# The front of a routed layer, rewritten as a loop in a held order, with rows gathered six tiles ahead and one-hots in 16 bits

## The chip, the core and the metric

The kernel runs on one core of a Trainium2 chip. The metric is device time in microseconds (us), the median of several executions. Engines are named as in the profile: PE is the matrix engine, PEld its weight loads, DVE the vector engine, ACT the scalar engine, POOL the one that issues the gathers here, and SP the one that issues most other DMAs. PEclk is the clock granted to PE as a share of full speed.

## What is computed

`x` has 32 items of 64 rows and 512 columns in fp32, that is 2048 rows, kept as NT = 16 tiles of 128 rows. Four layers follow each other, each of them `x = x + ffn(cond(x))`. What the change touches is the seam between layers 0 and 1:

```python
# layer 0, the end: a mixture of 7 experts, top 2, and a shared expert
shared = (silu(x @ sh_gate) * (x @ sh_up) / 8) @ sh_down
y0 = shared + sum(w[e] * expert_ffn(x, r_gate[e], r_up[e], r_down[e]) for e in range(7))
# layer 1, the start: a 64x64 mix per item, chosen by subject, then a router
c = einsum("bct,bcd->bdt", x, weights[subjects])
logits = c @ gate_w.T + gate_b          # 32 experts
topk_logits, topk_idx = top_k(logits, 4)
...
```

After this the rows of `c` are sorted by expert, each of the 32 experts works on its rows, and the results go back to their rows with softmax weights. Layer 2 (an adapter and a soft mixture) and layer 3 (paged attention and a quantised linear) come later and are not touched.

## The kernel before

`layer0` ends with its routed experts, which leave their rows in DRAM (`ys`). Behind a branch that treats rows beyond an expert's capacity, `layer1` (L1409) runs its front, a loop over the 16 tiles. For tile `i` it does this:

- `combined` (L1190) gathers two rows per row of the tile from `ys` (`gather`, L336, an indirect DMA that POOL issues) into `yk`, of which there are six buffers, and adds each to `x` with its gate (L1198, DVE). SP stores `x` to DRAM for later (L1430).
- One matmul with a block-diagonal weight mixes the items (L1432, into PSUM tile `mm`, 128x512). ACT copies it to `c` (L1436), and SP stores `c` to `rows` (L1437), from where the experts will gather.
- Four transposes of `c` go to `tp` (L1440), ACT copies them to `cT` (L1442), and four matmuls with `cT` as the stationary side and 32 moving columns make the router's logits `rp` (L1447). Four tiles share one PSUM bank for `rp`. DVE adds the bias (`lg`, L1449), and `choose` takes the largest eight values and their indices (L901, L902).
- The shared expert of layer 0 is still missing in six late tiles (8 to 13, the list `todo`). Its first part `up` (L481: 16 matmuls in fp32, which the hardware runs as 32) is in the even steps and `down` in the odd ones (L487: an identity matmul that brings `x` into PSUM at L492, two matmuls at L495, and a copy by ACT back over `x` at L496).
- `put` (L904) works on groups of tiles, given by `groups`: one step after the last tile of a group, it makes the place of every row among the rows of its expert. DVE makes a one-hot of the choice (`hot`), sums it (`sel`, L916) and accumulates it (`pre`, L918). Two matmuls give the rows ahead of each one (`at`, L921), and `placed` (L1238) turns a place into a tile number `tl` and a row `row`. From these, DVE makes two one-hot matrices `a` and `b` (L1254). ACT scales `a` by the row's number (L893, in `total`), four matmuls per tile sum a table of row numbers in PSUM (L895), and DVE adds the table to `tokens` (L896). The table, `at` and `fixed` are three stretches of one PSUM bank, `tok`.

When all 16 tiles are through, `end` (L1260) selects from `tokens` the row numbers of the two experts that have a fixed place (`fixed`). `m.ready` then starts to gather their rows (`xr<-rows,fixed`, L336), and `m.run` runs the experts. The weights of the first two experts are asked for just ahead of `end`, and `rest` (L1373) loads the tiles 8 to 15 of `x` in one go, at the start of the front.

The order of instructions on an engine is chosen by a scheduler from the dependences in the program. Only instructions that are pinned one by one hold the order in which the program issues them; in the front before, these are loads and a few others. The heart of the loop is:

```python
groups = {3: 4, 7: 4, 11: 4, 13: 2, 14: 1, 15: 1}
for i in range(NT):
    x = combined(sb, i, 3, bridge.x[i])
    nc.sync.dma_start(out=xs[i * P : (i + 1) * P, :], in_=x)
    o = ps.tile([P, D], F32, name="mm", tag="mm")
    nc.tensor.matmul(o, bridge.weights[i], x, start=True, stop=True)
    if i % 2 == 0 and i // 2 < len(todo):
        shared.up(sb, ps, todo[i // 2])
```

Of the kernel before, what the change touches and what calls it, by code (L numbers as in the profile page):

```python
# [2 lines left out]

# [38 lines left out]
LATER = range(6, NT - 2)  # L42
GAP = 2
# [35 lines left out]
def _consts():  # L79
# [14 lines left out]

    b["iota"] = np.tile(np.arange(P, dtype=f), (P, 1))
# [21 lines left out]
    d["same32"] = (p[:, None] % 32 == e).astype(f)  # L117
# [109 lines left out]

class Prog:


    def __init__(self, tc, a, ctx):
# [3 lines left out]
        self.named = {}  # L235
        self.constants(self.const, "cst")
# [222 lines left out]
class Shared:  # L459
# [12 lines left out]
    def up(self, sb, ps, i, tag="sh"):  # L472
# [13 lines left out]
        l0_expert(g, sb, self.acts[i], gu[:, 0:2, :], gu[:, 2:4, :], None)  # L486

# [290 lines left out]
class Moe:  # L778
# [297 lines left out]
    def run(self, xs, per_tile):  # L1076
# [138 lines left out]
        combined.fetch = fetch  # L1215
# [3 lines left out]
class Ranked(Moe):  # L1219
# [3 lines left out]
    def begin(self, sb, bank, at):  # L1223
        nc, g = self.g.nc, self.g
        self.bank, self.at = bank, at
        nc.vector.memset(self.pre[:, 0], 0.0)  # L1226
        self.tok = self.keep.tile([TC1, P], F32, name="tokens1")
        nc.vector.memset(self.tok, 0.0)
        self.room = self.keep.tile([P, 2, E1], F32, name="room1")
        self.widx = self.keep.tile([P, E1], I32, name="widx1")  # L1230
        self.each = self.keep.tile([P, E1], I32, name="each1")
        self.fixed = self.keep.tile([P, FIXED1 * 320 // P], I32, name="fixed1")
# [5 lines left out]
    def placed(self, sb, hot, i, n):  # L1238

        nc, iota, K = self.g.nc, self.g.c("iota"), self.K  # L1240
        fi, place = self.chosen[:, i : i + n, :], self.place[:, i : i + n, :]
        nc.vector.tensor_reduce(place, hot, AX.X, ALU.add)
        ai = sb.tile([P, n, K], I32, name=f"ai{n}")
        nc.vector.tensor_copy(ai, place)
        nc.vector.tensor_single_scalar(ai, ai, 7, ALU.arith_shift_right)
        tl = sb.tile([P, n, K], F32, name=f"tl{n}")
        nc.vector.tensor_copy(tl, ai)
        row = sb.tile([P, n, K], F32, name=f"row{n}")
        nc.vector.scalar_tensor_tensor(row, tl, -float(P), place, ALU.mult, ALU.add)
        nc.vector.scalar_tensor_tensor(tl, tl, 32.0, fi, ALU.mult, ALU.add)  # L1250
        a_ = sb.tile([P, n * K, TC1], F16, name=f"a_{n}", bufs=1)
        b_ = sb.tile([P, n * K, P], F16, name=f"b_{n}", bufs=1)
        for o, w, v in ((a_, TC1, tl), (b_, P, row)):
            nc.vector.tensor_tensor(  # L1254
                o, iota[:, 0:w].unsqueeze(1).to_broadcast([P, n * K, w]),
                v.rearrange("p n k -> p (n k)").unsqueeze(2).to_broadcast([P, n * K, w]), ALU.is_equal,
            )
        self.total(self.bank[0:TC1, 0:P], self.tok, a_, b_, a_, i, n)

    def end(self, sb):  # L1260

        g, nc, E, tok, ident = self.g, self.g.nc, self.E, self.tok, self.g.ident
        fixed = self.bank[:, 128:133]
# [97 lines left out]
class Bridge:  # L1361
# [11 lines left out]
    def rest(self, pool):  # L1373
        for i in range(NT):
            if i not in self.x:
                self.x[i] = self.g.load_x(pool, self.xs, i, NT - len(EARLY), True)
# [31 lines left out]

def layer1(g, bridge, combined, beside, w2):  # L1409
    tc, nc, a = g.tc, g.nc, g.a  # L1410
    with ExitStack() as ctx:
# [4 lines left out]
        with ExitStack() as c1:  # L1416
# [5 lines left out]
            bank, rps = (ps.tile([P, 512], F32, name=k, tag=k, bufs=1) for k in ("tok", "rp"))  # L1422
            m.begin(sb, bank, bank[:, 256:384])
            shared, todo = bridge.shared, list(LATER[GAP:])
            bridge.rest(wp)

            groups = {3: 4, 7: 4, 11: 4, 13: 2, 14: 1, 15: 1}
            for i in range(NT):
                x = combined(sb, i, 3, bridge.x[i])
                nc.sync.dma_start(out=xs[i * P : (i + 1) * P, :], in_=x)  # L1430
# [1105 lines left out]
```

## Time and profile before

| what | us |
|---|---|
| median of 3 runs | 2584.26 (2582.10 to 2585.11) |
| the profiled execution | 2621.27, of it 2619.4 in the span |
| layer 0 with its experts, to the branch | 0 to 599.9 |
| layer 1's front, which the change rewrites | 599.9 to 729.5 |
| layer 1's experts and what leads to layer 2 | 729.5 to 1230 |
| layers 2 and 3 | 1230 to 2619 |

PE is busy for 97.1 of the 129.6 us of the front, DVE for 73.5, ACT for 34.8 and POOL for 33.8, at a mean PEclk of 0.81. In all the other stages of the table PE is busy between 91 and 97 per cent of the time. The times of a stage come from the trace, whose span starts at 0; a row of the trace that reads `607.44 0.59 ACT L1436` starts at 607.44 us and lasts 0.59 us, and what stands in brackets at its end is the time for which the engine was idle just before, and what ended it.

### The profile page before, as it was taken

The page shows a single profiled execution, that of the slowest core. Times are in us where ns is not written, and L with a number is a line of the kernel's source. Part 1 is how long each engine was busy: PE and PEld are TensorE (multiplying, and loading weights), DVE is VectorE, ACT ScalarE, POOL GpSimd, SP SyncE. Part 2 cuts the span into 40 slices and gives each one's busy share as a digit, 9 for nine tenths or more (in the row PEclk, how much of TensorE's full clock was granted, in tenths as well). Part 3 has the DMA queues.
Part 4 walks back from the last instruction along what each step waited for, and adds up shares of the span by engine and source line. Part 5 has one row for each costly group of instructions (what it writes and reads, how often), then busy time and mean ns, then how long its engine had stood idle before and what let it go on. Part 6 is the DMA issues. An engine that isn't in the chain of part 4 may idle for free.

```text
span 2619.4 us, 42294 instructions
## 1 busy us (share of the span) xinstructions
PE 2460.3 (94%) x16512; PEld 1622.1 (62%) x16527; DVE 1413.2 (54%) x3457; ACT 723.7 (28%) x1513; POOL 901.5 (34%) x955
## 2 busy tenths in 40 slices
PE   6999989998789999978999999999999999979998
PEld 4777766666556666746666666666666665435554
DVE  4666646824645554436544444444444432658786
ACT  2445421112211111102222222222222221246664
POOL 2223226604044443523333333333333312564440
PEclk9999979998789999989999999999999999989999
DMA  2335235535356976844222222222222313524441
GB/s 101 114 119 181 87 107 181 185 130 189 136 165 224 361 272 242 292 130 147 68 74 71 71 71 71 72 74 75 71 73 72 95 54 133 166 64 125 129 145 44
DMA packets 132566, 339.34 MB, mean 130 GB/s; under 512 B 23993, under 2 KB 25049, under 8 KB 125056
## 3 DMA queue, kind: packets, MB, share of 16 engines
q1 hardware_dynamic: 90720, 188.83, 21.1%
q0 software_dynamic: 41056, 141.89, 17.3%
q10 hardware_dynamic: 576, 5.77, 0.5%
q8 instruction: 134, 2.20, 0.3%
q14 instruction: 80, 0.66, 0.1%
HBM read 245.21 MB, written 107.22 MB: 135 GB/s over the span
## 4 chain that ended last, share of the span: by engine, by line
PE 42%; DVE 9%; issue 1%; POOL 1%; DMA 1%; ACT 0%; ACTq 0%; POOLq 0%; SPq 0%; DVEq 0%
PE out L1909 9%; PE lp L1766 7%; PE gp L1898 3%; PE pp L2223 3%; PE zp L1843 3%; PE yp L1711 2%; PE hp L1875 2%; PE y L2471 2%; PE op L2449 2%; PE pT L2424 2%; PE sp L2402 1%; DVE xt L1213 1%; PE ep L1852 1%; DVE inv L1802 1%; PE kp L2375 1%
## 5 line engine op out<-in xcount | busy, mean ns | idle before, releaser
L1124 PE MATMUL gu<-xT,wt 128*128 128x320 f32 (+3 forms) x1472 | 396.8, 417 | 0.8 <-issue 0.8
L1124 PEld LDWEIGHTS gu<-xT,wt 128*128 128x128 f32 x1472 | 276.6, 192 | 120.5 <-issue 52.9
L1909 PE MATMUL out<-sb_w,gT 128*128 128x512 f32 x512 | 234.1, 600 | 10.3 <-DVE nn L1746 6.6
L1766 PEld LDWEIGHTS lp<-xnT,sb_mu 128*128 128x128 f32 x2048 | 234.8, 193 | 9.2 <-issue 6.7
L1766 PE MATMUL lp<-xnT,sb_mu 128*128 128x128 f32 x2048 | 237.8, 276 | 2.1 <-DVE xnT L308 1.4
L1843 PE MATMUL zp<-sb_w,xnT 128*128 128x512 f32 x512 | 228.4, 595 | 4.3 <-DVE z L1845 4.3
L1136 PE MATMUL y<-wt,hT 128*128 128x512 f32 (+2 forms) x544 | 201.2, 598 | 2.8 <-DVE yo L1144 2.2
L336 POOL DMA_INDIRECT kvst<-kv,gidx x96 | 96.6, 1006 | 279.0 <-DMA oldkv<-kvst 196.6
L1902 DVE COPY gT<-gp 128x512 f32<-128x512 f32 x64 | 44.3, 692 | 250.1 <-PE gp L1898 249.7
L1909 PEld LDWEIGHTS out<-sb_w,gT 128*128 128x128 f32 x512 | 93.6, 191 | 115.7 <-issue 95.5
L1843 PEld LDWEIGHTS zp<-sb_w,xnT 128*128 128x128 f32 x512 | 93.7, 190 | 112.2 <-issue 100.8
L336 POOL DMA_INDIRECT yk<-ys,slot x96 | 97.8, 1019 | 145.2 <-DVE pre L1226 74.2
L336 POOL DMA_INDIRECT kvt<-newkv,oidx x96 | 100.8, 1050 | 132.2 <-DMA kvt<-oldkv 73.0
L1880 ACT ACTIVATE h<-hp 128x512 f32<-128x512 f32 x128 | 69.5, 594 | 218.8 <-PE hp L1875 218.6
L1136 PEld LDWEIGHTS y<-wt,hT 128*128 128x128 f32 (+2 forms) x544 | 73.0, 167 | 65.5 <-issue 52.9
L336 POOL DMA_INDIRECT xr<-rows,stok x101 | 98.2, 973 | 44.2 <-issue 18.2
L774 POOL TENSOR_TENSOR ga<-ga,sg 128x288 f32<-128x288 f32 (+3 forms) x64 | 50.7, 793 | 169.3 <-ACT sg L770 168.2
L1920 POOL TENSOR_TENSOR xt<-xt,bc_bias 128x512 f32<-128x512 f32 x16 | 20.3, 1266 | 222.8 <-DMA x<-xt 208.9
L1771 DVE TENSOR_TENSOR lT<-lp,cmu 128x512 f32<-128x512 f32 x64 | 43.6, 680 | 93.7 <-PE lp L1766 93.7
L1804 POOL TENSOR_TENSOR eT<-eT,inv 128x512 f32<-128x512 f32 x64 | 71.8, 1124 | 55.1 <-DVE inv L1803 32.0
L1898 PEld LDWEIGHTS gp<-lT,h 128*64 128x64 f32 x2048 | 65.8, 139 | 38.7 <-issue 26.5
L1795 ACT ACTIVATE eT<-eT 128x512 f32<-128x512 f32 x64 | 40.4, 631 | 174.0 <-DVE eT L1792 151.8
(430 smaller groups left out, 4673.4 us busy)
## 6 DMA issues: line engine op xcount, KB each, us to landing
ys<-yo SPq DMA_DIRECT2D x106, 256.0 KB
oldkv<-kvst SPq DMA_DIRECT2D x96, 224.0 KB
kvt<-oldkv SPq DMA_DIRECT2D x96, 224.0 KB
ys<-zero SPq DMA_DIRECT2D x10, 2048.0 KB
xt<-x SPq DMA_DIRECT2D x62, 256.0 KB
x<-xt SPq DMA_DIRECT2D x48, 256.0 KB
wt<-w_e SPq DMA_DIRECT2D x7, 1536.0 KB
sb_w<-w SPq DMA_DIRECT2D x5, 1024.0 KB
```

The lines of the kernel that those rows point to most:

```text
L336: ins = self.nc.gpsimd.indirect_dma_start(out=out, out_offset=None, in_=src, in_offset=bass.IndirectOffsetOnAxis(ap=idx, axis=0), **kw)
L1124: follow(nc.tensor.matmul(o, wj[:, c, ic * P : (ic + 1) * P], xTs[u][:, c, 0:n], start=c == 0, stop=c == 3))
L1136: follow(nc.tensor.matmul(y[row : row + n, :], hTs[e][:, ic, col : col + n], wd[:, ic, :], start=ic == 0, stop=ic == 1,))
L1711: g.first(c, nc.tensor.matmul(yp, self.xT[:, c, :], w["w_2"][:, c, :], start=c == 0, stop=False))
L1766: g.first(e + c, nc.tensor.matmul(lp[:, e, :], w["mu"][:, c, (4 * q + e) * P : (4 * q + e + 1) * P], self.xnT[:, c, :], start=c == 0, stop ...
L1804: g.pin(nc.gpsimd.tensor_tensor(e3, e3, inv.unsqueeze(2).to_broadcast([P, 8, T]), ALU.mult))
L1843: g.first(c, nc.tensor.matmul(zp, self.xnT[:, c, :], w["w1"][:, c, cols], start=c == 0, stop=c == 3))
L1875: g.first(e + b, nc.tensor.matmul(hp[:, b, e, :], self.ews[q][r, e, :], self.z[q][r, e * P : (e + 1) * P], start=True, stop=True))
L1880: g.pin(nc.scalar.activation(self.hs[q][b], hp[:, b], AF.Gelu))
L1898: g.first(e + b + k, nc.tensor.matmul(gp[r, e, cols], self.hs[q][b][:, e, r], self.lT[q][:, e, cols], start=True, stop=True))
L1909: g.first(e, nc.tensor.matmul(self.out, self.gTs[q][:, e, :], w["w2"][:, 4 * q + e, :], start=q + e == 0, stop=q + e == 6 and q == 3))
L2223: nc.tensor.matmul(pp, xT[i][:, c, :], (w["w_kv3"] if z else wq)[:, c, :], start=c == 0, stop=c == 3)
```

## The change

The loop becomes a class, `Mixed`, whose `run` issues one step per tile and one more. What it issues goes through `g.held`, a wrapper which pins every instruction, so that each engine keeps the order of the program.

- **Gathers.** `fetch` asks for the two `yk` of a tile six tiles ahead (`LEAD`); there are 14 buffers. The adds of tile `s+1` and its store stand behind the mix of tile `s`.
- **Shared expert.** `pieces` cuts it into six pieces for each tile: four quarters of `up` and two halves of `down`. Three pieces go into each step until none is left. The identity matmul goes; ACT copies the result to `sht`, and POOL adds that to `x`.
- **Router.** For the tiles 0 to 10 (`SPLIT`), the weights are the stationary side, and the four partial products go side by side to the four column tiles of PE (`parts`, 32 rows each). ACT copies them, and one matmul with a constant (`same32`, which moves to another group of constants) sums them to `rp`. The other tiles use the form before.
- **Groups.** `put` is a generator that halts where its next part belongs to another engine; the loop takes it up again at given points. The last groups are {13: 2, 15: 2}. The one-hots are made from 16-bit operands in a layout with the choice `k` innermost, DVE scales `a` in place of ACT, and the tile number comes from adding and subtracting a large constant instead of integer steps. The sum over `k` becomes two adds.
- **Banks.** The table accumulates over all 16 tiles in a PSUM bank of its own. `at` (with `fixed`), `rp`, `parts`, `mm` and `tp` have one bank each, and the shared expert has two.
- **Loads.** `rest` loads one tile of `x` per step, two before the loop. The weights of the first two experts are asked for in the steps 10 and 12.

```diff
+LEAD = 6
+GROUPS = {3: 4, 7: 4, 11: 4, 13: 2, 15: 2}
+SPLIT = range(11)
...
+class Ordered:
+    def __getattr__(self, name):
+        issue = getattr(self.engine, name)
+
+        def ordered(*args, **kw):
+            ins = issue(*args, **kw)
+            self.g.pin(ins)
+            return ins
+
+        return ordered
...
+    def pieces(self, sb, ps, todo, x):
+        nc, w = self.g.held, self.w
+        gus, sgs, ys, acts = {}, {}, {}, {}
+        def up(i, q):
+            j, ic = q // 2, q % 2
+            if q == 0:
+                gus[i] = ps.tile([P, 4, P], F32, name="gu", tag="sh")
+            for c in range(4):
+                nc.tensor.matmul(
+                    gus[i][:, q, :], w["w_sh"][:, c, j * 256 + ic * P : j * 256 + ic * P + P], self.hT[i][:, c, :],
+                    start=c == 0, stop=c == 3,
+                )
+            if q == 3:
+                sgs[i] = sb.tile([P, 2, P], F32, name="sg")
+                nc.scalar.activation(sgs[i], gus[i][:, 0:2, :], AF.Sigmoid)
+        def act(i):
+            gu, sg = gus.pop(i), sgs.pop(i)
+            nc.vector.scalar_tensor_tensor(sg, gu[:, 0:2, :], 0.125, sg, ALU.mult, ALU.mult)
+            acts[i] = sb.tile([P, 2, P], F32, name="hT")
+            nc.vector.tensor_tensor(acts[i], gu[:, 2:4, :], sg, ALU.mult)
+        def down(i, ic):
+            if ic == 0:
+                ys[i] = ps.tile([P, D], F32, name="y", tag="sh")
+            nc.tensor.matmul(ys[i], acts[i][:, ic, :], w["w_shd"][:, ic, :], start=ic == 0, stop=ic == 1)
+            if ic:
+                t = sb.tile([P, D], F32, name="sht", bufs=2)
+                nc.scalar.copy(t, ys[i])
+                nc.gpsimd.tensor_tensor(x[i], x[i], t, ALU.add)
+        on_pe = []
+        for k, i in enumerate(todo):
+            for q in range(4):
+                if q == 2 and k:
+                    on_pe += [(partial(down, todo[k - 1], ic), None) for ic in range(2)]
+                on_pe.append((partial(up, i, q), partial(act, i) if q == 3 else None))
+        on_pe += [(partial(down, todo[-1], ic), None) for ic in range(2)]
+        return on_pe
...
-    def begin(self, sb, bank, at):
+    def begin(self, sb, ps):
         nc, g = self.g.nc, self.g
-        self.bank, self.at = bank, at
         nc.vector.memset(self.pre[:, 0], 0.0)
+        self.iota = sb.tile([P, P, K1], F16, name="iota16", bufs=1)
+        nc.vector.tensor_copy(self.iota, g.c("iota").unsqueeze(2).to_broadcast([P, P, K1]))
+        self.table = ps.tile([TC1, P], F32, name="table", bufs=1)
...
+    def put(self, sb, ps, i, n):
+        g, nc, K, E = self.g, self.g.held, self.K, self.E
         fi, place = self.chosen[:, i : i + n, :], self.place[:, i : i + n, :]
+        nc.vector.tensor_copy(fi, self.idx[:, i : i + n, 0:K])
+        shape = [P, n, K, E]
+        hot = sb.tile(shape, F32, name=f"hot{n}", bufs=2)
+        nc.vector.tensor_tensor(
+            hot, g.c("iota")[:, 0:E].unsqueeze(1).unsqueeze(1).to_broadcast(shape),
+            fi.unsqueeze(3).to_broadcast(shape), ALU.is_equal,
+        )
+        half = sb.tile([P, n, 2, E], F32, name=f"half{n}", bufs=1)
+        nc.vector.tensor_tensor(half, hot[:, :, 0:2], hot[:, :, 2:4], ALU.add)
+        sel = sb.tile([P, n, E], F32, name=f"sel{n}", bufs=2)
+        nc.vector.tensor_tensor(sel, half[:, :, 0], half[:, :, 1], ALU.add)
+        for j in range(n):
+            nc.vector.tensor_tensor(self.pre[:, i + j + 1], self.pre[:, i + j], sel[:, j], ALU.add)
+        at = ps.tile([P, 4, E], F32, name="at", bufs=1)[:, 0:n]
+        yield "tensor"
+        nc.tensor.matmul(at, g.ones, self.pre[:, i : i + n], start=True, stop=False)
+        nc.tensor.matmul(at, g.c("upper"), sel, start=False, stop=True)
+        yield "vector"
+        nc.vector.tensor_tensor(hot, hot, at.unsqueeze(2).to_broadcast(shape), ALU.mult)
         nc.vector.tensor_reduce(place, hot, AX.X, ALU.add)
+        tile_ = sb.tile([P, n, K], F32, name=f"tile{n}", bufs=2)
+        nc.vector.tensor_scalar(tile_, place, 1.0 / P, 0.5 / P - 0.5, ALU.mult, ALU.add)
+        nc.vector.tensor_scalar(tile_, tile_, MAGIC, MAGIC, ALU.add, ALU.subtract)
+        row = sb.tile([P, n, K], F16, name=f"row{n}", bufs=2)
+        nc.vector.scalar_tensor_tensor(row, tile_, -float(P), place, ALU.mult, ALU.add)
+        tl = sb.tile([P, n, K], F16, name=f"tl{n}", bufs=2)
+        nc.vector.scalar_tensor_tensor(tl, tile_, 32.0, fi, ALU.mult, ALU.add)
+        yield "vector"
+        a_ = sb.tile([P, n, TC1, K], F16, name=f"a_{n}", bufs=2)
+        b_ = sb.tile([P, n, P, K], F16, name=f"b_{n}", bufs=2)
+        for o, w, v in ((b_, P, row), (a_, TC1, tl)):
+            to = [P, n, w, K]
             nc.vector.tensor_tensor(
+                o, self.iota[:, 0:w].unsqueeze(1).to_broadcast(to), v.unsqueeze(2).to_broadcast(to), ALU.is_equal
             )
+        for j in range(n):
+            nc.vector.tensor_scalar(a_[:, j], a_[:, j], g.c("tok")[:, i + j : i + j + 1], None, ALU.mult)
+        yield "tensor"
+        for j in range(n):
+            for k in range(K):
+                nc.tensor.matmul(
+                    self.table, a_[:, j, :, k], b_[:, j, :, k], start=i + j + k == 0,
+                    stop=i + j == NT - 1 and k == K - 1,
+                )
...
+    def end(self, ps):
+        g, nc, tok, ident = self.g, self.g.held, self.tok, self.g.ident
+        nc.vector.tensor_copy(tok, self.table)
+        fixed = ps.tile([P, FIXED1 * 320 // P], F32, name="fixedp", tag="at", bufs=1)
...
-    def rest(self, pool):
-        for i in range(NT):
-            if i not in self.x:
-                self.x[i] = self.g.load_x(pool, self.xs, i, NT - len(EARLY), True)
+    def rest(self, pool, i):
+        if i < NT and i not in self.x:
+            self.x[i] = self.g.load_x(pool, self.xs, i, NT - len(EARLY), True)
...
+class Mixed:
...
+    def fetch(self, i):
+        if i >= NT:
+            return
+        g, m = self.g, self.before
+        self.yk[i] = [self.sb.tile([P, D], F32, name="yk", bufs=K0 * (LEAD + 1)) for _ in range(K0)]
+        for k, yk in enumerate(self.yk[i]):
+            g.gather(yk, m.ys, m.slot[:, i, k : k + 1], later=True)
+    def adds(self, i):
+        if i >= NT:
+            return
+        g, x = self.g, self.bridge.x[i]
+        for k, yk in enumerate(self.yk.pop(i)):
+            g.held.vector.scalar_tensor_tensor(x, yk, self.before.gates[:, i, k : k + 1], x, ALU.mult, ALU.add)
+        g.held.sync.dma_start(out=self.xs[i * P : (i + 1) * P, :], in_=x)
+    def mix(self, i):
+        nc = self.g.held
+        o = self.ps.tile([P, D], F32, name="mm", bufs=1)
+        nc.tensor.matmul(o, self.bridge.weights[i], self.bridge.x[i], start=True, stop=True)
+        self.c[i] = self.sb.tile([P, D], F32, name="c")
+        nc.scalar.copy(self.c[i], o)
+        nc.sync.dma_start(out=self.m.rows[i * P : (i + 1) * P, :], in_=self.c[i])
+    def turn(self, i):
+        nc, c = self.g.held, self.c.pop(i)
+        tp = self.ps.tile([P, 4, P], F32, name="tp", bufs=1)
+        for cc in range(4):
+            nc.tensor.transpose(tp[:, cc, :], c[:, cc * P : (cc + 1) * P], self.g.ident)
+        self.cT[i] = self.sb.tile([P, 4, P], F32, name="cT", bufs=2)
+        nc.scalar.copy(self.cT[i], tp)
+    def route(self, i):
+        nc, cT = self.g.held, self.cT.pop(i)
+        if i not in SPLIT:
+            self.rp[i] = self.ps.tile([P, E1], F32, name="rp", bufs=1)
+            for cc in range(4):
+                nc.tensor.matmul(self.rp[i], cT[:, cc, :], self.wr[:, cc, :], start=cc == 0, stop=cc == 3)
+            return
+        parts = self.ps.tile([P, P], F32, name="parts", bufs=1)
+        for cc in range(4):
+            nc.tensor.matmul(parts[32 * cc : 32 * cc + 32], self.wr[:, cc, :], cT[:, cc, :], start=True, stop=True)
+        self.parts[i] = self.sb.tile([P, P], F32, name="partss", bufs=2)
+        nc.scalar.copy(self.parts[i], parts)
+    def logits(self, i):
+        if i in SPLIT:
+            self.rp[i] = self.ps.tile([P, E1], F32, name="rp", bufs=1)
+            self.g.held.tensor.matmul(self.rp[i], self.parts.pop(i), self.g.c("same32"), start=True, stop=True)
+    def choose(self, i):
+        lg = self.sb.tile([P, E1], F32, name="lg")
+        self.g.held.vector.tensor_tensor(lg, self.rp.pop(i), self.br, ALU.add)
+        self.m.choose(i, lg)
+    def run(self):
+        g, m, bridge, puts = self.g, self.m, self.bridge, []
+        todo = list(LATER[GAP:])
+        for i in todo[:2]:
+            bridge.rest(self.wp, i)
+        pieces = bridge.shared.pieces(self.sb, self.ps, todo, bridge.x)
+        def acts():
+            while self.late:
+                self.late.pop(0)()
+        def fill(n=1):
+            for piece, late in pieces[:n]:
+                if len(pieces) <= 2:
+                    acts()
+                piece()
+                if late:
+                    self.late.append(late)
+            del pieces[:n]
+        def go(engine):
+            for put in list(puts):
+                if put[1] == engine:
+                    put[1] = next(put[0], None)
+                    if put[1] is None:
+                        puts.remove(put)
+        for i in range(LEAD):
+            self.fetch(i)
+        fill(4)
+        self.adds(0)
+        for s in range(NT + 1):
+            self.fetch(s + LEAD)
+            bridge.rest(self.wp, todo[0] + 2 + s)
+            if s < NT:
+                self.mix(s)
+            self.adds(s + 1)
+            fill()
+            if s:
+                self.logits(s - 1)
+            if s < NT:
+                self.turn(s)
+            acts()
+            if s:
+                self.choose(s - 1)
+            fill()
+            go("tensor")
+            go("vector")
+            if s == NT - 1:
+                go("vector")
+            if s < NT:
+                self.route(s)
+            fill()
+            if s - 1 in GROUPS:
+                puts.append([m.put(self.sb, self.ps, s - GROUPS[s - 1], GROUPS[s - 1]), "vector"])
+                go("vector")
+            if s in (10, 12):
+                m.weights((s - 10) // 2)
+        while puts:
+            go("tensor")
+            go("vector")
+        assert not pieces
+        m.end(self.ps)
...
+            m.begin(sb, ps)
+            Mixed(g, sb, ps, wp, m, combined.moe, bridge, wr, br, xs).run()
```

## The prediction

> **What bounds the stage.** I read first the page's engine row (PE 94% busy over the span), then a table by stage, which says where PE is not busy. The changed code runs from 599.9 us (first instruction behind the branch that closes layer 0) to 729.5 us (first row gather of layer 1's experts). All times of the trace are us from the span's start.
>
> ```profile
> span 2619.4 us, 42294 instructions
> ...
> PE 2460.3 (94%) x16512; PEld 1622.1 (62%) x16527; DVE 1413.2 (54%) x3457; ACT 723.7 (28%) x1513; POOL 901.5 (34%) x955
> ```
>
> ```profile
> core 0: us, PE busy (x) PEld busy (x) DVE busy (x) ACT busy (x) POOL busy (x), PEclk, DMA share, GB/s
> 599.90:624.50 24.60, 15.36 (x66) 10.18 (x66) 9.28 (x19) 4.11 (x8) 16.16 (x16) 0.80 0.75 231
> 624.50:676.50 52.00, 50.69 (x324) 39.95 (x323) 32.49 (x89) 15.29 (x28) 17.62 (x16) 0.96 0.53 177
> 676.50:708.70 32.20, 24.24 (x124) 17.76 (x124) 20.92 (x65) 12.75 (x22) 0.00 (x0) 0.76 0.39 150
> 708.70:729.50 20.80, 6.85 (x37) 5.58 (x36) 10.80 (x41) 2.61 (x5) 0.00 (x1) 0.50 0.22 74
> ```
>
> Four parts, four limits: a start with a hole in it; a middle where PE is full; a late part with holes and a PE clock of 0.76; and 20.8 us after the last expert choice in which PE is busy 6.85 us at half clock. In the last part one short chain runs, three times over: one-hots on DVE, their scaling on ACT, the table's matmuls, the add into `tokens`, and only then the next group's prefix sums, because all of them share one PSUM bank. Two turns of it in the timeline:
>
> ```profile
> 719.45 0.68 DVE L1254 TENSOR_TENSOR b<-sb_cst,row 128x512 f16<-128x512 f32 x1
> 720.05 0.55 DVE L1254 TENSOR_TENSOR a<-sb_cst,tl 128x384 f16<-128x384 f32 x1
> 720.64 0.61 ACT L893 ACTIVATE a<-a,sb_cst 128x384 f16<-128x384 f16 x1 [5.20 <-DVE a L1254]
> 721.30 0.45 PEld L895 LDWEIGHTS <-a 128*96 128x96 f16 x4 [3.85 <-ACT a L893]
> ...
> 722.00 0.28 DVE L896 TENSOR_TENSOR tokens<-tokens,tok 96x128 f32<-96x128 f32 x1 [1.40 <-PE tok L895]
> 722.34 0.50 PEld L921 LDWEIGHTS tok<-pre,sb_cst 128*128 128x128 f32 x2 [0.59 <-DVE tokens L896]
> ...
> 729.50 0.95 POOL L336 DMA_INDIRECT xr<-rows,fixed  x1 [57.66 <-DVE yo L1293]
> ```
>
> The hole of the start is one wait, on ACT, and PE stands behind it:
>
> ```profile
> 607.44 0.59 ACT L1436 COPY c<-mm 128x512 f32<-128x512 f32 x1 [2.42 <-issue]
> 616.72 0.59 ACT L1442 COPY cT<-tp 128x512 f32<-128x512 f32 x1 [8.70 <-DMA yk<-ys,slot]
> 617.36 1.78 PEld L1447 LDWEIGHTS rp<-sb_w_r,cT 128*128 128x128 f32 x8 [8.05 <-issue]
> ```
>
> The copy's source (tp) was done by 609.3, so the releaser named is not its producer. The DMA view has no packet of an instruction queue between 602 and 616, and one at 616 to 617, with the DMA engines at a share near 0.95 (gathers): I read the wait as an instruction fetch of ACT that came late. PE's clock is then 0.50 from 616.7 to 628.0 (windows).
>
> [...] 2048 elements took 2288 ns, 1536 took 1752. For 16 bits no row exists[...] The trace has such matmuls in layer 2: 32 of `csum` (128\*32) in 1.08 us against 8 of `rp` in 0.97 us. [...] Here PE stood from 676.5 to 680.5 and the clock was 0.50 for 680 to 688. [...]
>
> **PE prices** (full clock, from start to start in the timeline of 630 to 641): mm 0.86 us for 512 columns; four transposes tp 0.45; rp 0.89; an up quarter 32/4 = 8 instructions of 0.113 = 0.90; one half of down 0.86. Before, two tiles took 630.24 to 640.91 = 10.67, that is 5.33 a tile, with nothing idle.
>
> **Part by part.**
>
> *Shared expert.* Three pieces a step, as before (six per two tiles), so 3 x 0.89 = 2.67. The identity matmul (L492, 0.9 us per tile of six) goes: -5.4 us of PE. In its place ACT copies to `sht` (0.59, as for L496) and POOL adds it to x (1.27, as L1920 has it). POOL then has 2 gathers x 1.25 + 0.7 = 3.2 us a step, hidden.
>
> *Router as column tiles, 11 steps.* rp 0.89 becomes parts, 8 of 0.03 = 0.25, and logits, 2 of 0.11 = 0.22; with two drains of 0.2 about 0.15 saved. ACT gets one copy of 128x128 (0.25, as L2452).
>
> *A step.* 0.86 + 2.67 + 0.45 + 0.47 + 0.2 = 4.65 us; the puts' share is (0.45 + 16 x 0.09)/4 = 0.47 a tile. Sum 5.1, I take 5.05. ACT's waits fit: turn needs mix + 0.2 + 0.59, and PE has 1.1 us of fill and logits there; route needs 1.33 from the turn's start, and has 0.45 + 0.90.
>
> *DVE.* Two adds 2 x 0.75 and gaps = 1.57; choose (0.19 + 0.19 + 0.09 + 0.19 and gaps) 0.75; the activation 0.88 every other step. A put of four: cast, hot, half, sel, four pre = 0.18 + 0.69 + 0.42 + 0.29 + 0.88 = 2.6 with gaps (the reduce of 1.05 goes); hot x at, place, four small = 2.3; one-hots 1.22 + 0.96 and four scalings of about 0.2 = 3.0. Sum 7.9, before 9.3 and 2.13 on ACT. Per tile 1.57 + 0.75 + 0.44 + 2.0 = 4.8: just below PE. If 16 bits bring nothing: 2.29 + 1.75 + 4 x 0.46 = 5.9, per tile 5.5, so DVE would set the pace. Below nothing it can't go: the elements stay. I take the fast value. A mix needs its adds, which stand first in the step before: from logits (1.8 us into a step) through choose, the longest piece and the next adds is 1.8 + 0.75 + 3.0 + 1.57 = 7.1 of the 10 us that two steps give.
>
> *Table in a bank of its own.* The `tokens` add (0.28) and the wait between groups go. The table's operands are read with a stride of 8 bytes, of which the trace shows nothing[...]. I take 0.09.
>
> *Gathers six tiles ahead.* 12 gathers go out back to back, 600.3 to 615.3. Tile 1 was in by 608.0 before; the loop needs it by 611. Later tiles have slack, so DVE's waits for yk (13.7 us in sum) go. In the first 30 us the queues carry 24 gathers, 12 stores and six of the x loads (SP had all eight x loads out by 566; now six stand in the loop): 42 x 0.26 MB = 11 MB, 365 GB/s, more than the 320 to 340 seen. Stores and loads slip, which costs nothing with this lead; an instruction fetch may slip too.
>
> **The sum.** First mix at 606.3 as before (it hangs on the first two gathers, landed at 604.1 and 605.4). Eleven steps of 5.05, less one piece: 661.0. Steps 11 to 14 have no pieces and run the chain mix 0.86 + 0.2, copy 0.59, tp 0.7, copy 0.59, rp 0.94 = 3.9, say 4.0: step 15 starts at 677. DVE is behind there (step 14 has adds 1.57, choose 0.75, 3.0 and the next group's 1.75): choose(15) ends 8.0 us into step 15. Then for the last two tiles 1.75, prefix sums 1.4 at half clock, 1.6, 1.65, table 1.5, copy, four selecting matmuls and fixed 2.0: 17.9. With 1 us for lag the first row gather is at **696**, were the start clean: 33.5 us early.
>
> *The start's hole.* Nothing in the change alters how many ACT instructions precede the branch, and DMA is loaded at least as much. If it stays, step 1 begins at 616.7 + 1.35 and not at 611.4 (+6.7), and 11.3 us at clock 0.50 cost up to 5.6, say 4.8. So 696 + 11.5 = **707.5, 22 us early**. Behind the gather the program is as before. The experts' first two weights are asked for at steps 10 and 12, not at 700.5; no wait on them showed. Profiled: 2621.27 - 22 = 2599.3. The three timed runs have a median of 2584.26, 37 below the profiled execution; I carry the difference over unscaled: **2562**.
>
> **Cases.**
>
> A, the hole stays (0.47): 2562, own range 2556 to 2568.
>
> B, the hole goes, since the queue order puts the fetch elsewhere (0.24): gain 33.5, 2551. For: eight of the x loads' bytes lie elsewhere. Against: 12 gathers run then, as now.
>
> C, 16 bits bring nothing and the late steps run at half clock (0.16): 11 x 0.4, tail +1.5 + 0.7, five steps of up to 2.2 half the time 5.5; gain 22 - 12 = 10, 2574. For: late steps have PE at work only 2.2 of 4 us. [...]
>
> D, slower (0.08): the held order makes DVE and PE wait for each other in turn (choose behind logits, the next adds behind a put piece, mix behind adds). Its point: 16 steps at a mean of 4.7 now; at 617.8 + 16 s + 13.8 + 1 = 729.5, s = 6.1 is break-even. At 6.5 us a step it costs +6.5 us, 2591. Against: the 2.9 us of slack above.
>
> E, no change that can be told (0.05): C and D in part.
>
> Faster by over 0.2% (5.2 us, about what a measurement tells from no change) 0.87, within 0.05, slower 0.08. The range leaves out D, E, C's upper part and B's lower tail: 2545 to 2577.
>
> **What would show it.** Right: adds without waits for yk; steps of 5.0 between mm starts; b of 2048 at 1.2 us; 18 to 20 us from the last mm to the row gather; that gather at 705 to 710. Case B: no ACT wait over 3 us before 620. Wrong: b at 2.29 us (C); mm starts 6 us apart with DVE full (D); or the row gather early and the experts' first matmul not.

## The result and the profile after

The changed kernel takes 2561.99 us (2559.63 to 2563.60, 4 runs) beside 2583.18 us for the kernel before (2578.96 to 2585.11): a ratio of 0.9919, 95% interval 0.9902 to 0.9937, so 21.2 us less. The forecast was 2562.

One thing has to be known to read the numbers: executions fell on chips of two kinds. On kind F the kernel before takes 2580 to 2583 us (medians), and layer 2, which the change does not touch, takes 904 to 906 us from its first to its last matmul of `lp`; on kind S these are 2619 to 2620 and 928 to 933. The profiled execution of before (2619.4, layer 2: 928.2) was of kind S, the one of after is of kind F. The 58 us between the two spans are thus no gain; 23 of them lie in layer 2 alone. Only what lies before the first row gather is compared below.

The page of after, and its table by stage (columns as before: length, busy time and instructions of each engine, PEclk, DMA share, GB/s):

```profile
span 2561.5 us, 42341 instructions
...
PE 2442.1 (95%) x16533; PEld 1612.1 (63%) x16533; DVE 1405.8 (55%) x3456; ACT 718.3 (28%) x1508; POOL 905.8 (35%) x961
```

```profile
core 0: us, PE busy (x) PEld busy (x) DVE busy (x) ACT busy (x) POOL busy (x), PEclk, DMA share, GB/s
599.90:624.50 24.60, 22.55 (x156) 17.29 (x155) 12.35 (x29) 7.52 (x16) 19.25 (x20) 0.93 0.91 308
624.50:657.00 32.50, 32.50 (x238) 23.97 (x237) 26.03 (x76) 12.11 (x26) 20.33 (x18) 1.00 0.75 251
657.00:684.00 27.00, 20.82 (x96) 13.70 (x95) 22.26 (x60) 6.71 (x12) 1.35 (x1) 0.76 0.63 215
684.00:705.00 21.00, 12.39 (x65) 9.95 (x64) 10.79 (x46) 2.71 (x4) 0.96 (x1) 0.50 0.21 60
```

The start has PE busy for 22.55 of 24.60 us, where before had 15.36: the hole is not there in this execution. The middle is full. What is left is the end: from 657 on, PE runs at a clock of 0.76 and then 0.50, and DVE is busy for 22.26 of 27 us. The late steps can be read from ACT's copies of tiles 12 to 15, one in each step, beside the clock (same columns as above):

```profile
669.75 0.59 ACT L242 COPY c<-mm 128x512 f32<-128x512 f32 x1 [2.99 <-PE mm L242]
...
673.83 0.59 ACT L242 COPY c<-mm 128x512 f32<-128x512 f32 x1 [2.11 <-PE mm L242]
...
680.13 0.59 ACT L242 COPY c<-mm 128x512 f32<-128x512 f32 x1 [3.87 <-PE mm L242]
...
686.44 0.59 ACT L242 COPY c<-mm 128x512 f32<-128x512 f32 x1 [3.87 <-PE mm L242]
```

```profile
670.00:674.20 4.20, 2.67 (x14) 1.61 (x14) 3.89 (x13) 1.29 (x3) 0.00 (x0) 1.00 0.61 168
674.20:684.00 9.80, 8.13 (x29) 5.98 (x29) 7.35 (x21) 1.97 (x4) 0.00 (x0) 0.50 0.71 251
```

At full clock the step is 4.08 us long, at half clock 6.30 and 6.31. The front ends here (timeline of after: start, length, engine, line, operation; L242 is the wrapper that pins):

```profile
699.18 0.69 DVE L242 TENSOR_TENSOR b<-iota,row 128x1024 f16<-128x1024 f16 x1
699.79 0.55 DVE L242 TENSOR_TENSOR a<-iota,tl 128x768 f16<-128x768 f16 x1
700.38 0.55 DVE L242 TENSOR_SCALAR a<-a,sb_cst 128x384 f16<-128x384 f16 x2
...
701.95 0.29 DVE L242 COPY tokens<-table 96x128 f32<-96x128 f32 x1 [1.02 <-PE table L242]
702.29 1.02 PEld L242 LDWEIGHTS fixedp<-sb_cst,tokens 96*128 96x128 f32 x8 [0.61 <-DVE tokens L242]
...
703.87 0.96 POOL L360 DMA_INDIRECT xr<-rows,fixed  x1 [38.99 <-DMA bc_adapt<-adapt]
```

There is one turn of one-hots, table and selection behind the last choice and not three in a row; the turn of tiles 12 and 13 has its one-hots at 692.5, before the last choice ends (694.8). The first row gather stands at 703.87, 25.6 us before that of the profile before. From this gather to layer 2's first matmul both take nearly the same (456 and 459 us).

To see which part of the front gained, I cut it at the copies `c<-mm` of ACT, of which there is one per tile: c0 to c15 is the loop, c15 to the first row gather is the tail. Since layer 0 doesn't end at the same time in every execution (the first gather of `yk` starts between 595.3 and 602.1 us), the last column counts from that gather to the first row gather.

| run | kind | c0 to c1 | c0 to c15 | tail | first row gather | from first `yk` |
|---|---|---|---|---|---|---|
| before, profile shown | S | 10.7 | 92.1 | 30.0 | 729.5 | 129.2 |
| before, again | S | 2.9 | 87.1 | 30.0 | 721.9 | 123.9 |
| after, the result | F | 6.1 | 80.2 | 17.4 | 703.9 | 104.6 |
| after, again | F | 4.5 | 79.8 | 17.5 | 699.6 | 104.3 |
| after, again | S | 15.5 | 94.1 | 17.4 | 714.4 | 119.0 |

The tail is 12.5 us shorter in each of these executions of the changed kernel. Its loop is shorter only in the two on kind F, whose start is clean. The kernel before has no profile on kind F, so how much of the loop's gain is the change and how much the chip can't be read from the table. Within kind S the front is 5 to 10 us shorter, and the medians are 10.9 us apart (experiment 5).

### The profile page after: what moved, and what is told of

Read it like the earlier page. It is cut to its first block, busy times and chain, and to the rows that moved or that the text cites. A ratio compares the mean times of both kernels' runs of the same rounds, so it can differ in the third digit from the quotient of the medians.

```text
span 2561.5 us, 42341 instructions
## 1 busy us (share of the span) xinstructions
PE 2442.1 (95%) x16533; PEld 1612.1 (63%) x16533; DVE 1405.8 (55%) x3456; ACT 718.3 (28%) x1508; POOL 905.8 (35%) x961
## 4 chain that ended last, share of the span: by engine, by line
PE 50%; DVE 3%; POOL 1%; issue 1%; DMA 1%; ACT 0%; POOLq 0%; ACTq 0%; DVEq 0%; SPq 0%
PE out L2107 9%; PE lp L1964 9%; PE zp L2041 7%; PE pp L2421 3%; PE hp L2073 3%; PE gp L2096 3%; PE y L2669 2%; PE yp L1909 2%; PE op L2647 2%; PE pT L2622 2%; PE sp L2600 2%; PE ep L2050 1%; PE kp L2573 1%; PE ap L1897 1%; PE csum L2060 1%
## 5 line engine op out<-in xcount | busy, mean ns | idle before, releaser
L2611 ACT ACTIVATE s<-s,m 128x336 f32<-128x336 f32 x128 | 72.8, 570 | 57.3 <-DVE m L2607 56.1
L1969 DVE TENSOR_TENSOR lT<-lp,cmu 128x512 f32<-128x512 f32 x64 | 43.5, 680 | 80.2 <-PE lp L1964 80.2
L2052 ACT COPY ew<-ep 128x512 f32<-128x512 f32 x64 | 37.6, 589 | 177.0 <-PE ep L2050 177.0
```

The costliest lines, as they stand in the source:

```text
L2611: nc.scalar.activation(p, p, AF.Exp, bias=m, scale=-1.0, accum_out=tot)
```

## The experiments

Each expectation was written before its kernel ran. All times of a front are those of one profiled execution; ratios are to the kernel before on the same chip.

**1. The kernel before, once more (kind S).**

> The kernel before, unchanged, profiled once more. Theory: the ACT wait of 8.7 us at the front's start is bound to the place of the instructions in the program; then it is there again (over 6 us between 605 and 618 us), the first row gather comes at 729.5 within 2 us, and the 37 us by which the first profiled execution was longer lie behind the front, in layer 2 and later: a span near 2582. Rival: the hole belongs to one execution; then this one has no ACT wait over 3 us there, and the first row gather comes at 716 to 722.

Median 2619.14 against 2618.88, ratio 1.0002 [0.9989, 1.0015]. Neither theory holds as put. ACT waits again at the start (5.45 us at L496, 2.29 us at L1442), but at other instructions, and the gather comes at 721.9, which is in the rival's range although the rival's condition, no wait over 3 us, is not met. The front of one and the same program differs by 7.6 us between two executions. The span did not fall to 2582 either: all 12 runs of it took 2614.5 to 2628.4 us, so the 37 us go with the chip and not with one execution.

**2. One-hots from fp32 operands (kind S).**

```diff
-        self.iota = sb.tile([P, P, K1], F16, name="iota16", bufs=1)
+        self.iota = sb.tile([P, P, K1], F32, name="iota16", bufs=1)
...
-        row = sb.tile([P, n, K], F16, name=f"row{n}", bufs=2)
+        row = sb.tile([P, n, K], F32, name=f"row{n}", bufs=2)
...
-        tl = sb.tile([P, n, K], F16, name=f"tl{n}", bufs=2)
+        tl = sb.tile([P, n, K], F32, name=f"tl{n}", bufs=2)
```

> The changed kernel with iota, row and tl in fp32, so that both one-hots have fp32 operands; their results stay in 16 bits. Theory (16 bits keep DVE below PE's pace): b of 2048 goes from 1.21 to 2.29 us and a of 1536 from 0.95 to 1.75; a group of four costs 1.9 us more, DVE about 5.3 us a tile against PE's 5.08, and the first row gather goes from 703.9 to 707 to 712. Rival (DVE has slack in the full steps and only the last two groups count): 0.9 us twice, 705.5 to 706. Second rival: the operands' type does nothing, b stays at 1.2 us and the gather at 704.

The groups of DVE by shape, of after and of this kernel (busy us, mean ns):

```profile
L242 DVE TENSOR_TENSOR b<-iota,row 128x2048 f16<-128x2048 f16 x3 | 3.6, 1206 | 0.0
...
L242 DVE TENSOR_TENSOR a<-iota,tl 128x1536 f16<-128x1536 f16 x3 | 2.9, 950 | 0.0
```

```profile
L242 DVE TENSOR_TENSOR b<-iota,row 128x2048 f16<-128x2048 f32 x3 | 6.8, 2273 | 0.0
L242 DVE TENSOR_TENSOR a<-iota,tl 128x1536 f16<-128x1536 f32 x3 | 5.3, 1753 | 0.0
```

The type halves the operation (2273 to 1206 ns, 1753 to 950), as forecast. The gather came at 718.9, behind a start with a stall (c0 to c1: 15.7 us), so it is set against after on kind S, which has the same stall: loop 95.3 against 94.1, tail 18.9 against 17.4, 2.7 us together. That lies between the rival (1.6 to 2.1 us) and the theory (3.1 and more): most of the full steps hide it. Only the tail's 1.5 us is a clean comparison, because the loops of the two executions also have short stalls at different steps. The ratio is 0.9982 [0.9969, 0.9995] beside 0.9962 [0.9949, 0.9975] for after on that kind.

**3. Gathers two tiles ahead, not six (kind S).**

```diff
-LEAD = 6
+LEAD = 2
```

> The changed kernel with the gathers two tiles ahead in place of six, so with six yk buffers as before. Theory (two steps of 5 us cover the 5 us of a gather's way): first row gather within 1.5 us of 703.9, and DVE waits for yk of under 10 us in sum (6.7 with six ahead). Rival (the lead is what removes the stalls): the waits come to over 15 us and the gather to 712 or later.

Ratio 0.9924 [0.9902, 0.9945], gather at 705.5. DVE's waits, of this kernel:

```profile
DVE xt L242 <- DMA yk<-ys,slot: 10.1, 10, 2.2
```

10.1 us in ten waits, none over 2.2 us, and the gather 1.6 us behind 703.9: both at the edge of what I expected, and the rival falls. The lead of six is not what removes the stalls. On the contrary, of the six forms of the changed kernel profiled on kind S this is the only one whose start was clean: c0 to c1 took 5.6 us and the loop 85.0, against 15.5 and 94.1 for after there. That is one execution, and it isn't free of such waits: in step 6 the transposes end at 633.92 by the records, and ACT's copy of them starts at 636.17.

**4. Nothing pinned (kind S).** The wrapper's engines are replaced by the engines themselves:

```diff
-            k: Ordered(self, getattr(self.nc, k)) for k in ("tensor", "vector", "scalar", "gpsimd", "sync")
+            k: getattr(self.nc, k) for k in ("tensor", "vector", "scalar", "gpsimd", "sync")
```

> The changed kernel with nothing pinned beyond what was pinned before: the scheduler chooses the order of the same instructions. Theory (the held order is what keeps PE full at 5.08 us a step): the steps stretch, and the first row gather comes 6 to 20 us later than 703.9. Rival (banks, gathers and pieces bring the gain, and the scheduler finds an order as good): within 2 us of 703.9.

The theory falls, and in the other direction. The gather came at 710.8 although the start stalled here too (c0 to c1: 16.1 us). From c1 to the gather it takes 88.3 us; after takes 96.0 on kind S, of which 4.4 are stalls between 642 and 657 us, and 91.6 and 92.7 on kind F. Ratio 0.9930 [0.9913, 0.9946]. The late steps of this kernel in the timeline:

```profile
685.41 0.66 PE L1547 MATMUL tp<-sb_cst,c 128*128 128x128 f32 x4 [0.68 <-ACT c L1540]
685.90 1.02 PE L1538 MATMUL mm<-xt,wbd 128*128 128x512 f32 x2
686.16 0.59 ACT L1549 COPY cT<-tp 128x512 f32<-128x512 f32 x1 [0.80 <-PE tp L1547]
...
686.80 1.08 PE L1557 MATMUL rp<-sb_w_r,cT 128*128 128x32 f32 x8
686.96 0.59 ACT L1540 COPY c<-mm 128x512 f32<-128x512 f32 x1 [0.22 <-PE mm L1538]
```

The scheduler puts the next tile's mix (mm) between the transposes and the router of this one. Each of ACT's two copies then has a matmul beside it, and the step is 2.2 us long here (copies of c at 684.77 and 686.96). Not all are as short: the four steps from c11 to c15 take 15.6 us, against 21.7 for after on kind S. In the held order the router stands before the next mix, so PE and ACT take turns.

**5. After, unchanged (kind S), and 6. with matmuls that nobody reads (kind S).**

```diff
+    def warm(self, n):
+        t = self.ps.tile([P, P], F32, name="parts", bufs=1)
+        for _ in range(n):
+            self.g.held.tensor.matmul(t, self.g.ident, self.g.ident, start=True, stop=True)
...
+            if s < NT and s > 10:
+                self.warm(3)
             if s < NT:
                 self.turn(s)
...
+            if s < NT and s > 10:
+                self.warm(3)
             if s < NT:
                 self.route(s)
...
         while puts:
+            self.warm(6)
             go("tensor")
```

> The changed kernel, unchanged, on the chip on which the kernel before takes 2619. Theory (the late releases of PE's waiters at the front's start come in one execution and not in another, and with the lead of two they came in none): either the start is clean again and the first row gather stands at 702 to 706, or ACT waits once or twice for 5 to 12 us before 622 and the gather stands at 711 to 719; the ratio to before is 0.992 as before, with runs that spread by over 8 us. Rival (the start of this kernel is always clean): gather at 702 to 706 and all runs within 5 us.

> The changed kernel with matmuls that nobody reads (identity by identity, into the PSUM bank of the column tiles, which is free after step 10): three ahead of the transposes and three ahead of the router in each step from 11 on, six in each turn of the tail. Theory (the late steps of 5.9 us and the tail of 19.6 us are a chain of PE and ACT that runs at half clock): PEclk stays at 1.00 through 657 to 705, the late steps take 4.5 to 5 us, and the first row gather comes 5 to 9 us earlier than in a_again with an equally clean start; the time falls by 6 to 11 us. Rival (DVE sets the late steps): the clock rises, the late steps stay above 5.5 us, and the gather moves by less than 2 us.

After has a ratio of 0.9962 [0.9949, 0.9975] here, 10.9 us, and not the 21.2 of the result. Its start (timeline):

```profile
604.12 1.06 PE L242 MATMUL tp<-sb_cst,c 128*128 128x128 f32 x4
...
612.53 0.59 ACT L242 COPY cT<-tp 128x512 f32<-128x512 f32 x1 [9.08 <-remote]
...
618.23 0.27 ACT L242 COPY partss<-parts 128x128 f32<-128x128 f32 x1 [5.11 <-PE y L242]
```

In the result's execution the same copy starts 0.08 us behind its transposes (608.66 and 608.74). Here the records of the transposes end at 605.18 and the copy starts at 612.53. ACT's wait names the semaphore of PE and that of a DMA queue. In the result's execution the same wait passes at 608.70, with the last update of the DMA's semaphore at 595.56, so the DMA it asks for lies ahead of the front; in experiment 5 that semaphore was last updated at 591.90 before the wait began. This leaves PE's, whose update the trace has at 612.46. "Remote" in brackets means that no engine of the trace ended just then. The expectation for after, a gather at 711 to 719 with a stall, is met; that its runs spread by over 8 us is not (2605.72 to 2612.81).

With the unread matmuls the table by stage is

```profile
657.00:684.00 27.00, 24.85 (x176) 18.01 (x175) 20.81 (x53) 9.37 (x19) 8.43 (x7) 1.00 0.54 187
684.00:705.00 21.00, 19.61 (x141) 16.44 (x139) 18.28 (x60) 5.98 (x9) 0.00 (x0) 1.00 0.55 189
```

The clock is 1.00 in both stretches. The steps from c11 to c15 take 4.55 us each, against 5.41 in experiment 5 and in the result's execution. From c1 to the gather it takes 88.8 us against 96.0 in experiment 5; 5.0 of these 7.2 us lie between c10 and c15, and 1.9 are shorter stalls before c10. The tail, in which the clock now stays at 1.00 until 706.2, takes 17.1 us against 17.4, so the theory falls there. The gather itself came at 715.8, since this start stalled for longer (c0 to c1: 20.0 us). Ratio 0.9938 [0.9915, 0.9961]. The median is 6.3 us below after's, but the six runs lie between 2595 and 2612 us and after's six between 2606 and 2613, so on the time of the whole kernel this gain is not shown.

**7. The router in its old form in all steps (kind S).**

```diff
-SPLIT = range(11)
+SPLIT = range(0)
```

> The changed kernel with the router in its old form in all steps (four matmuls with 32 moving columns). Theory (PE sets the pace of the steps 0 to 10): each of them takes 0.15 to 0.42 us longer, so mm starts 5.2 to 5.5 us apart in place of 5.08, and the first row gather comes 1.7 to 4.6 us later with an equally clean start. Rival (DVE sets it): under 1 us.

Between c3 and c10 the steps take 5.31 us each; after on kind F has 5.06 there. That is the 0.25 us that the theory gives. On the whole nothing can be told: 0.9958 [0.9946, 0.9971] against 0.9962, and 96.0 us from c1 to the gather in both. Each has stalls of its own there: 8.6 us from c1 to c2 here, and 642 to 657 us in after on kind S.

**8. The first 12 gathers as plain loads (kind F).**

```diff
+            if i < LEAD:
+                at = (2 * i + k) * P
+                g.held.sync.dma_start(out=yk, in_=m.ys[at : at + P, :])
+            else:
+                g.gather(yk, m.ys, m.slot[:, i, k : k + 1], later=True)
-            g.gather(yk, m.ys, m.slot[:, i, k : k + 1], later=True)
```

> The changed kernel in which the 12 gathers ahead of the loop (tiles 0 to 5) are plain loads of the same size from ys, issued by SP: each tile gets rows 128 by 128 in order and not those of its own choice, so what comes after the front differs too, and only the front's times are read. Theory P (PE's waiters are released late while POOL issues gathers back to back): no ACT wait of over 3 us at the start whose source was done, mm copies 0 and 1 at most 7 us apart, and the first row gather at 698 to 706. Rival D (the DMA traffic of the start does it, whoever issues it): a wait of 5 to 14 us stays, and the gather comes at 711 or later.

**9. Lead of two and unread matmuls together (kind F).**

> Both edits that gained: gathers two tiles ahead in place of six, and the matmuls that nobody reads in steps 11 and later. Theory (the two gains lie in different stretches and add): clean start as in a_lead2, late part as in a_warm, first row gather at 696 to 700, time 23 to 27 us below before (ratio 0.990 to 0.991), that is 5 to 9 us below a_lead2 and 10 to 16 below the changed kernel on such a chip. Rival (a_lead2's clean start was one execution's luck): ratio 0.993 to 0.995 like a_warm.

The start of 8 is clean (c0 to c1: 6.3 us, gather at 706.6). But the chip was of kind F, where after's start is clean as well, so it tells nothing. Experiment 9 has the gather at 698.6 and a loop of 77.3 us, the shortest of all; its ratio of 0.9924 [0.9904, 0.9943], 20.0 us below before where 23 to 27 were expected, is no better than the result's.

**10 to 12. After, 8 and 9 again on one chip (kind F).**

> The changed kernel again, as the control of the two kernels that run beside it on one chip. If the chip is of the kind that runs the kernel before at about 2619: a wait of over 5 us at the start whose source was done, the first row gather at 711 to 719, ratio 0.996. If it is of the kind that runs it at about 2582: a clean start, gather at 702 to 706, ratio 0.992.

> The kernel with the first 12 gathers as plain loads by SP once more (the rows of tiles 0 to 5 are not those of their own choice), on the same chip as the changed kernel. Theory P (POOL's back-to-back gathers hold up the release of PE's waiters): a clean start, mm copies 0 and 1 at most 7 us apart, also where the changed kernel beside it stalls. Rival D (the traffic does it, and the clean start seen so far was the chip's): it stalls where the changed kernel stalls, mm copies 0 and 1 over 10 us apart.

> Lead of two and unread matmuls in the late steps, on the same chip as the changed kernel. Theory: first row gather at 697 to 700 with a clean start; 10 to 16 us below the changed kernel where that one stalls at its start, 4 to 7 us below it where it doesn't. Rival (the unread matmuls cost later what they gain in the front): within 3 us of the changed kernel where that one has a clean start.

| run | ratio | median | loop | tail |
|---|---|---|---|---|
| after | 0.9918 [0.9902, 0.9934] | 2559.07 | 79.8 | 17.5 |
| plain loads | 0.9947 [0.9933, 0.9961] | 2567.41 | 82.8 | 17.4 |
| lead of two, unread matmuls | 0.9912 [0.9896, 0.9927] | 2559.03 | 77.5 | 18.1 |

All three start clean, so the cause of the stalls stays open. The two edits together are not faster than after on kind F: their loop and tail together are 1.7 us shorter, which the runs can't tell from nothing; the rival of that expectation holds. What they would bring together on kind S was not tried. Of the two alone there, the lead of two has a ratio whose interval just clears that of after (0.9902 to 0.9945 against 0.9949 to 0.9975, on two chips), and the unread matmuls' does not.

## Why the prediction was right, and where it was not

The time and its sign are right, and so are the sum's large terms. The way to them was partly not: a hole was kept that did not come, and other terms were priced too low. These errors largely cancel, so that the forecast of 2562 met 2561.99 so closely is luck; the row gather, put at 705 to 710, came at 703.9.

- **Steps 0 to 10 at 5.05 us.** c1 to c10 takes 44.8 us for nine steps in the result's execution, 4.97 each. A step without matmuls of a `put` takes 4.67 us, where the terms (three pieces, mm, tp, router in parts) give 4.65. The price of the column tiles, taken from layer 2's `csum` in the profile before (32 matmuls in 1.08 us), agrees with experiment 7 (0.25 us a step). Step 10 does not fit: from its mm to that of step 11 it takes 7.30 us where the sum has 4.16. PE waits there for DVE from 657.01 to 659.16, and its clock is 0.50 from 660.59 to 664.00.
- **Gathers.** The adds were to be without waits for yk. They keep 6.7 us of the 13.7, all of it at the start.
- **16 bits.** 1.22 and 0.96 us were my estimate; the profile before has 1.219 and 0.951 us for half the elements in fp32 (L1254, 128x1024 and 128x768). 1.206 and 0.950 were measured, with operands that are broadcast as here. Case C's first half falls. Its price, given as 11 times 0.4 and 1.5 in the tail, was too high in the loop: 1.2 there and 1.5 in the tail (experiment 2).
- **The tail.** From mm of step 15 (684.35) to the gather 19.5 us, forecast 17.9 and 1. Of three turns behind the last choice one is left; this is the gain that no execution lacks. Which edit brings it was not taken apart: the table's own bank, the merged last groups and DVE's scaling of `a` came together, and only the 16 bits were tried alone (1.5 us).
- **The start's hole: wrong reading, and the likelier case did not come.** I took "an instruction fetch of ACT that came late" from a packet of an instruction queue at 616 us and let it stay (11.5 us). In after such a packet comes at 615.1 and ACT does not wait. Such a packet comes 14 to 17 us behind the first gather in twelve of the fourteen traces, stalled or not. What ACT waits for last is PE's semaphore: in the profile before, its update is at 616.65, and the transposes had ended by 609.3. The result's start is that of case B. On kind S it is like that of case A, with 15 to 20 us between c0 and c1 for all five kernels with a lead of six, where 6 are normal. So the starts of A and B both came, on chips of different kinds; the profile of before could not tell, and the time of 2562 is that of kind F, where the start is B's.
- **The late steps: the mis-sized term.** "3.9, say 4.0" assumed PE at full clock, and there it holds: step 12 takes 4.08 us from mm to mm. But the steps 11 to 14 take 21.1 us and not 16. Step 11 also has 16 matmuls of the table, which the chain leaves out (1.3 us more), and PEclk falls to 0.50 at 674.2, which makes the steps 13 and 14 3.7 us longer. I had given such a fall little weight, and that was an estimate: in the 4.2 us before it PE was busy for 2.67, in short pieces with no gap over 0.73 us, and the clock fell. Experiment 6 shows the price: kept busy, the last three steps take 4.1 to 4.2. This half of case C, late steps at half clock for 5.5 us, did come.
- **The baseline.** 729.5 was one execution; the other has 721.9.

Put together: case B's clean sum had the gather at 696. What comes before step 11 adds 2.3 (step 10 3.1, the rest gains 0.8), the steps 11 to 14 add 5.1, the tail 0.6: 704, as measured. My forecast had 707.5 because it kept a hole of 11.5 and missed those 7.4 and 0.6. Against a front of 721.9 to 729.5 before, that is a gain of 18 to 26, and 21.2 was measured; but these two fronts are of kind S and the 21.2 of kind F, so this agreement is no proof.

The rivals: D (steps of 6.1 us by mutual waiting) didn't come. Its mechanism, a held order in which PE and others wait in turn, is there in the late steps: experiment 4 shows the scheduler's order 3 to 4 us shorter behind the start than the clean executions of after, so pinning is not shown to be a source of the gain, and may be a cost; this compares single executions on two kinds of chip.

Two things were not settled. Why PE's semaphore comes late at the start: it happens while POOL issues gathers without a break (595.4 to 615.5 in experiment 5), and not at the start of the kernel with a lead of two, whose first run of gathers ends at 606.8. But on kind F the same run of gathers stands, DMA moves as much (275 GB/s from 599.9 to 617 in the result's execution, 281 in experiment 5), and nothing is late. Set side by side, the copies of the transposes (`cT<-tp`) for which ACT stood idle started over 1 us behind the end of their transposes at least once in each of the eight traces of kind S, the kernel with a lead of two included (1.3 us at its start, 2.2 in step 6), and in none of the six of kind F. The kind of chip parts them without exception; the lead does not. Whether the gathers' issue, their traffic, or something else on those chips holds it up stays open, since plain loads ran on kind F alone. The recording of the profile is a rival too that no run here tests: at the stalls some updates of PE's semaphore are missing from the record (in experiment 5 the one that lets the copy at 602.86 go). And the kernel before has no profile of kind F.

## What to carry to other kernels

Look for short chains that run several times in a row because they share one buffer, here a PSUM bank: the tail, in which such a chain stood three times and now stands once behind the last choice, took 30.0 us in both profiles before and 17.4 after on both kinds of chip (by all its edits together), while the loop took 80 us on one kind and 94 on the other. Before pricing a step at PE's full clock, look at how much PE has to do in it: here the clock fell to 0.50 behind 4.2 us with PE busy for 2.67, and with the unread matmuls of experiment 6, where PE was busy for 24.85 of 27 us and 19.61 of 21, it stayed at 1.00. A step can be filled with the next tile's independent matmul, as the scheduler did by itself in experiment 4 (a step of 2.2 us). And do not put a wait down to an event because the two are close in time; look for the same event in a trace without the wait.

## What was not expected of the hardware

- PE's clock fell to 0.50 with PE busy for 2.67 of the 4.2 us before, and stayed there for 41 us (674.24 to 715.20). No gap in those 4.2 us was over 0.73 us. The front of after has two earlier falls, at 605.98 and 660.59, with a gap of 2.05 and of 2.15 us in the 4 us before them; in the profile before, PE had stood for 3.0 us when the clock fell at 679.48.
- Semaphore updates of PE came 2 to 13 us later than the end of its matmul in the records, in the traces of kind S alone, and several at once: in experiment 2 four came between 620.17 and 620.29 us, for matmuls whose records end between 612.9 and 618.3.
- The changed kernel's layer 2 took 905 us on one chip and 928 on another (the result's execution and experiment 5), at nearly the same mean PE clock over the span (0.974 and 0.973).
